# The head of a two-layer AdaLN/FFN kernel on one Trainium2 core: convolutions done directly, the first matrix loaded by another queue, end columns computed between rows of the first product

## The chip, the cores and the metric

The kernel runs on one core of one Trainium2 chip. The metric is device time in microseconds, from launch to the end of the execution. The kernel before was timed in four runs: 958.36, 963.05, 961.65 and 954.70 us, median 960.0 us.

## The reference, cut to what matters

The input is 32 samples of 64 channels and 1024 columns. Two layers follow one another. Each layer modulates the input with a small four-stage convolution net whose weights depend on a style vector, feeds the result to a matrix product, and adds that to its input:

```python
for i, typ in enumerate(('same', 'upsample', 'same', 'downsample')):
    s = style @ mw.T + mb                       # 32 x 64
    weight = SCALE * w * s[:, None, :, None]
    demod = rsqrt(sum(weight * weight, axis=(2, 3)) + EPS)
    weight = weight * demod[:, :, None, None]   # 3 taps, 64 -> 64 channels, one set per sample
    out = conv(out, weight) + b                 # 'same': 3 taps, pad 1; the two others blur as well
...
x = x + L0_ffn(L0_cond(x, cond))   # scores, top 16 of 64 experts, rank-16 products A and B
x = x + L1_ffn(L1_cond(x, cond))   # 1024 x 1024 product with int4 weights
```

In layer 0 the product with `A` (1024 x 1024) and with the router `Wr` (1024 x 64) is one product with a matrix of `AW` = 1088 columns. The 16 best scores of 64 gate its result before the product with `B`.

## The kernel before, in words

Two samples make a pair: its 2 x 64 channels lie in 128 partitions, and they are the 128 rows of the pair's token matrix. There are `NP` = 16 pairs, and every pair goes through the same stages in each layer.

**The convolution net of one sample.** The four stages are folded into two. `first` is the first convolution. A sample's 1024 columns lie twice in 128 partitions, once shifted, so that one product covers two taps. Before, a sample is first turned by `differences` into a middle part scaled by the style and two differences with its neighbours (one ACT and two DVE instructions that read every fourth column, L637 to L641). `first` then makes three products (L659, L665), moves the middle one out with ACT (`yt`, L661), joins the other two to it on DVE (L666), takes further differences on DVE (L671) and differences of these on POOL (L674). All this saves products in `rest`, which is the second, third and fourth stage composed into one: six products into one bank (L701, L709), two additions on DVE (L717, L723), four products into a second bank (L732), and a sum on DVE. The weights of `rest` are made per pair: `composed1` (`r`, then `g`, L546 to L568) and `composed2` (`f`, L579; copies L594 to L597; sums of them L599, L605).

**The product of layer 0.** `layer0` multiplies the token matrix `th` of a pair (8 chunks of 128 rows) with the 8 blocks of A. The blocks are split into high and low parts (`split_weights`, L148, L351 to L353: DVE, POOL and ACT work for each block), and every later pair uses three products of these parts. The first two pairs, `WHOLE = (0, 1)`, use A as it was loaded in plain f32 (`araw`), so that the splits can be made beside them. Their 24 products of 352 or 368 columns run block by block (`ks`), with places (`yield`) between the blocks where other work is put: `later` is `rest` of the next pair, `conv` is `first` of the pair after it.

**The ends.** The composed weights are not right for the outermost columns. `ends` computes these for all 16 pairs at once from eight columns at each side (`xg`), in a chain `xe`, `ye`, `ue`, `ze`, `ve`, `bt`, `re`, `rt`, in which TensorE and VectorE take turns. The result goes to DRAM (`red`). For pairs 0 and 1 `outer` puts it into rows 0 and 127 of `th`, in chunks 0, 1, 6 and 7, by DMA; for the others `re` is read back and merged in `rest`.

**The head.** Everything before the first product of pair 2 is written out by hand at the bottom of the function: the order there, with `tc.issue_after(...)` as anchors, is the order in which the engines get their instructions; each engine runs its own list in order. `factors` makes style, demodulation and tables; `rows` and `tbl` spread two rows of each sample over the partitions (L326, L331, L341). SP (SyncE) issues the loads of x and the small loads, POOL issues the loads of A (L365, L366). `araw` lies in rooms 5 to 7 of the weight blocks, pair 1's `y` in room 4, and the scratch of `ends` in room 2, which block 2 of the split A takes later.

Of the kernel before, what the change touches and what calls it, by code (L numbers as in the profile page):

```python
# [62 lines left out]
def adaln_ffn_kernel(ctx: ExitStack, tc: tile.TileContext, t, out: bass.AP):  # L63
# [90 lines left out]
    WHOLE = (0, 1)  # L154

# [166 lines left out]
    def last_rows(i, k, v):  # L322


        ps = mpst(f"rows{i}_{k}")
        nc.tensor.transpose(ps[:B, :C], v[:C], ident[:C, :C])  # L326
        nc.scalar.copy(rows[:, k], ps[:B, :C])
        if i == 0:
            ps = fpst(f"rows{i}_{k}b")[:, : 4 * C].rearrange("p (n c) -> p n c", n=4)
            for n in range(4):  # L330
                nc.tensor.matmul(  # L331
                    ps[:, n],
                    ident[:B, n : n + 1].to_broadcast([B, P]),
                    rows[:, k],
                    start=True,
                    stop=True,
                )
            for p in WHOLE:
                if k == 0:
                    tbl[i, p] = wk.tile([P, 2, 2, C], F32, tag="tbl", name=f"tbl{i}_{p}", bufs=3)  # L340
                nc.scalar.copy(tbl[i, p][:, :, k], ps[:, 2 * p : 2 * p + 2])  # L341


    def split_weights(raw, w, ks, into, name):

        for k in ks:
            ws = block(k, [P, 3, w], F32R, f"{name}{k}")
            for c in range(0, w, H):
                cs = slice(c, min(c + H, w))
                h = high(raw[k][:, cs], f"{name}h{k}_{c}")  # L350
                nc.gpsimd.tensor_tensor(ws[:, 1, cs], raw[k][:, cs], h, ALU.subtract)  # L351
                nc.scalar.copy(ws[:, 0, cs], h)  # L352
            nc.vector.scalar_tensor_tensor(  # L353
                ws[:, 2], ws[:, 1], -RADIX, ws[:, 0], ALU.mult, ALU.add
            )
            into.append(ws)

    def load_a():

        raw = []  # L360
        wr = t["wrT"].rearrange("(s q) e -> s q e", q=NC)
        av = t["aT"].rearrange("(s q) f -> s q f", q=NC)
        for n, (a, b) in enumerate(((0, 3), (3, 6), (6, 8))):
            r = block(5 + n, [P, 3, AW], F32, f"araw{n}")
            nc.gpsimd.dma_start(r[:, : b - a, :E], wr[:, a:b])  # L365
            nc.gpsimd.dma_start(r[:, : b - a, E:], av[:, a:b])  # L366
            raw += [r[:, j] for j in range(b - a)]
        return raw
# [40 lines left out]
    def ends(i, lo, hi, room, behind=()):  # L409
# [92 lines left out]
        if i == 1:  # L502
            yield
# [10 lines left out]
        if i == 1:  # L514
            yield
# [55 lines left out]
    def composed2(i, p, g):  # L571

        ps = mpst(f"f{i}_{p}")
        pv = ps.rearrange("p (n c) -> p n c", n=4)
        gv = g.rearrange("p k h c -> p k (h c)")
        steps = ((3, 1, 0), (1, 2, 0), (5, 0, 0), (4, 1, 1), (2, 2, 1), (0, 3, 1))
        for m, (e, n, k) in enumerate(steps):
            v = gv[:, 0::2] if k == 0 else gv[:, 1:2]
            done["f"] = nc.tensor.matmul(  # L579
                pv[:, n : n + 2 - k],  # L580
                iw[:, e].rearrange("p a b -> p (a b)"),
                v,
                start=(m == 0),
                stop=(m == len(steps) - 1),
                skip_group_check=True,
            )
        pv = ps.rearrange("p (n h c) -> p n h c", n=4, h=2)
        fw = []
        for h in range(2):

            f = fwv(h)
            once = i == 0 and p == 0
            f8 = f[:, : 8 * C].rearrange("p (k c) -> p k c", c=C)
            nc.scalar.copy(f8[:, 0::2], pv[:, :, h])  # L594
            copy = nc.vector.tensor_copy if once else nc.scalar.copy
            copy(f8[:C, 1::2], pv[C:, :, h])
            copy(f8[C:, 1:7:2], pv[:C, 1:, h])  # L597
            v = f[:, : 4 * P].rearrange("p (a two b) -> p a two b", two=2, b=P)
            (nc.vector if once else nc.gpsimd).tensor_tensor(  # L599
                f[:, 4 * P : 6 * P].rearrange("p (a b) -> p a b", b=P),  # L600
                v[:, :, 0],
                v[:, :, 1],
                ALU.add,
            )
            done["sum"] = nc.gpsimd.tensor_tensor(  # L605
                f[:, 6 * P :], f[:, : 2 * P], f[:, 2 * P : 4 * P], ALU.add
            )
            fw.append(f)
        return fw
# [12 lines left out]
    def load_x(i, n):  # L622


        if i == 0:
            xd = xdv(n)
            src = t["x"][n // 2, halves[n % 2], :]
            nc.sync.dma_start(xd[:C, 2 : L + 2], src)
            done["x"] = nc.sync.dma_start(xd[C:, 1 : L + 1], src)
            return xd[:, 2 : L + 3 : 4], xd[:, 0 : L + 1 : 4], xd[:, 4 : L + 1 : 4]  # L630
# [20 lines left out]
    def first(i, n, y):  # L651

        a = al0[:, n : n + 1]
        xe = xev(n)
        w = c0 if i == 0 else xdv(n)[:, : 3 * P].rearrange("p (a b) -> p a b", a=3)
        mid = cpst(f"c{i}_{n}_1")[:, :HQ]
        nc.tensor.matmul(mid, w[:, 1], xe[:, :HQ], start=True, stop=True)  # L659
        yt = wk.tile([P, HQ], F32, tag="yt", name=f"yt{i}_{n}", bufs=2)  # L660
        nc.scalar.activation(yt, mid, AF.Identity, bias=be0[:, n : n + 1], scale=a)  # L661
        yb, yo = y[:, :HQ], y[:, YO : YO + HQ + 1]
        for q, w_, d, o in ((0, HQ, yb, 2 * HQ - 1), (2, HQ - 1, yo[:, 1:HQ], HQ)):
            ps = cpst(f"c{i}_{n}_{q}")[:, :w_]
            done["c"] = nc.tensor.matmul(ps, w[:, q], xe[:, o : o + w_], start=True, stop=True)  # L665
            nc.vector.scalar_tensor_tensor(d, ps, a, yt[:, :w_], ALU.mult, ALU.add)  # L666
        nc.vector.memset(yb[:C, 0:1], 0.0)
        nc.vector.memset(yb[C:, HQ - 1 : HQ], 0.0)
# [4 lines left out]
        for k in range(2):  # L673
            nc.gpsimd.tensor_tensor(  # L674
                e[:, :, k], d[:, :, 2 * k : 2 * k + HQ - 2 : 2], d[:, :, 1 : HQ - 1 : 2], ALU.subtract
            )
        return y

    def rest(i, n, y, f):
# [12 lines left out]
        both = wk.tile([P, 4 * HQ], F32, tag="rt", name=f"rt{i}_{n}", bufs=1)  # L692
# [3 lines left out]

        d = y[:, YD:YO].rearrange("p (a b) -> p a b", a=2)
# [42 lines left out]
        def shape(v):  # L740
            return v.rearrange("p (k c) -> p k c", c=C)

        if whole:
            done["r0"] = nc.vector.tensor_tensor(th, shape(ps), shape(both[:, :H]), ALU.add)
            return
# [70 lines left out]
    def layer0(p, ws):  # L816
# [52 lines left out]
        if whole:  # L869


            three = [chunk(c) for c in range(3)]
            ks = (2, 3, 4, 5, 0, 1, 6, 7) if p == 0 else tuple(range(NC))
            for n, k in enumerate(ks):
                for ch in three:
                    product(ch, key, ws, at, Q, (k,), ks[0], ks[-1])
                if n in (1, 2, 4, 5, 6):
# [191 lines left out]
    def load(k, h=None):  # L1069
        if k < len(todo):  # L1070
            i, p = todo[k]
            for h in range(2) if h is None else (h,):
                xin.setdefault(k, []).append(load_x(i, 2 * p + h))
# [9 lines left out]
    def begin(k):  # L1083
        if k < len(todo):
# [11 lines left out]
    def conv(k, h, y=None):  # L1096
        if k < len(todo):
            i, n = todo[k][0], 2 * todo[k][1] + h
            y = yv(n) if y is None else y
            ys.setdefault(k, []).append(first(i, n, y))  # L1100
# [16 lines left out]
    nc.sync.dma_start(condT, t["condT"])  # L1117
    zeros_once()
    set0 = factors(0, *(block(k, [P, 3 * AW], F32, f"room{k}") for k in range(2)))
    next(set0)  # L1120
    clear(0)
    room4 = block(4, [P, 3 * AW], F32, "room4")
    y1 = [room4[:, h * Y : (h + 1) * Y] for h in range(2)]
    clear_y([yv(0), yv(1)] + y1)
    load(0)
    with tc.issue_after(done["x"].ins):
        for s, c in enumerate((0, L - 8)):
            nc.sync.dma_start(xg[:, :, s], t["x"][:, :, c : c + 8].rearrange("n p w -> p n w"))
    for _ in range(2):
        next(set0)  # L1130
    with tc.issue_after(done["blur"].ins):
        begin(0)
        compose(0)
        for h in range(2):
            conv(0, h)
    anchors = [done["xe"]]
    load(1)
    weights(0)
    with tc.issue_after(done["f"].ins):
        next(set0)  # L1140
    with tc.issue_after(done["sum"].ins):
        araw = load_a()
    with tc.issue_after(done["f"].ins):
        begin(1)
        compose(1)
        for h in range(2):
            conv(1, h, y1[h])
    with tc.issue_after(done["c"].ins):
        run(set0)
    set_ends = ends(0, 0, NP, block(2, [P, 3 * AW], F32, "room2"), anchors)  # L1150
    for h in range(2):
        next(set_ends)
        later(0, h)
        anchors.append(done["r0"])
    run(set_ends)
    outer(0)
    load(2)
    tables_of(2)
    behind = [done[v].ins for v in ("re", "r0")]
    with ExitStack() as stack:  # L1160
        for v in behind:
            stack.enter_context(tc.issue_after(v))
        weights(1)

    wa, wb, braw = [], [], []
    for k in range(NP):
# [4 lines left out]
        if k + 2 < NP:  # L1171
# [12 lines left out]
        if k == 0:  # L1184
            with ExitStack() as stack:
                for v in behind:
                    stack.enter_context(tc.issue_after(v))
                split_weights(araw, AW, range(5), wa, "wa")
        if k + 3 < NP and not ahead:
            load(k + 3)  # L1190
            tables_of(k + 3)
        beside = [[] for _ in range(5)]
        if not ahead and not last:
            beside[1] += [(later, k + 1, 0)]
            beside[3] += [(later, k + 1, 1)]
            if k + 2 < NP:
                beside[2] += [(conv, k + 2, 0), (compose, k + 2)]
                beside[4] += [(conv, k + 2, 1)]
        if k == 1:
# [159 lines left out]
```

## Time and profile before

| what | value |
|---|---|
| median of four runs | 960.0 us (954.7 to 963.05) |
| the profiled execution, its own time | 958.36 us |
| span of its instructions | 956.6 us |
| PE (TensorE matmul) busy | 884.9 us, 93% of the span |
| DVE (VectorE) | 725.9 us, 76% |
| POOL (GpSimd) | 470.1 us, 49% |
| ACT (ScalarE) | 323.8 us, 34% |
| first load of A issued, first product of pair 0 started | 29.7 us, 44.9 us |
| first product of pair 2 (split A) started | 135.7 us |

How to read it: times are microseconds from the start of the span. PE is the engine that does the products, PEld its weight loads, which overlap. A line such as L806 is a line of the kernel. In a list of waits, "PE r L701 <- POOL cv L599" says that TensorE's product at L701 stood still until POOL's instruction at L599 was done. PEclk is the share of its full clock that TensorE was granted. An f32 product counts as two instructions.

### The profile page before, as it was taken

The numbers are of one execution on the slowest core, as the hardware profiler recorded it, in microseconds if no ns is written. First come the engines' busy times: TensorE is split into PE (matmuls) and PEld (weight loads), VectorE is DVE, ScalarE is ACT, GpSimd is POOL, SyncE is SP. The second block draws the span as 40 slices with busy tenths as digits, with TensorE's granted clock in tenths as the row PEclk, the third lists the DMA queues.
The fourth block names the chain that finished last, engine by engine and source line by source line (L and its number), as shares of the span: only waits on it lengthen the run. The fifth ranks groups of instructions, "written<-read, shape, count | busy, mean of one in ns | idle before, by whom it ended". The sixth has DMA issues, their size and how long they took to land.

```text
span 956.6 us, 14770 instructions
## 1 busy us (share of the span) xinstructions
PE 884.9 (93%) x5069; PEld 785.8 (82%) x5069; DVE 725.9 (76%) x1505; ACT 323.8 (34%) x702; POOL 470.1 (49%) x601
## 2 busy tenths in 40 slices
PE   5778879999999999999999999988899999989996
PEld 4656669999999999984778887778899899988886
DVE  6856886878877788657986666588878887888885
ACT  4224442443443333332332221263233323332320
POOL 4455463444555544455662221334756655665563
PEclk9898989999999999999999999999999999999999
DMA  5721121222222221344455655464323332333221
GB/s 122 234 59 50 50 70 52 83 80 76 72 72 82 91 87 68 111 172 128 150 201 201 223 198 197 157 220 134 105 89 103 103 122 90 105 100 122 83 84 44
DMA packets 48443, 109.81 MB, mean 115 GB/s; under 512 B 12580, under 2 KB 20896, under 8 KB 48368
## 3 DMA queue, kind: packets, MB, share of 16 engines
q1 hardware_dynamic: 46208, 103.42, 34.7%
q0 software_dynamic: 1200, 4.46, 1.4%
q10 hardware_dynamic: 960, 0.99, 0.4%
q8 instruction: 40, 0.66, 0.3%
q14 instruction: 35, 0.29, 0.1%
HBM read 70.97 MB, written 37.88 MB: 114 GB/s over the span
## 4 chain that ended last, share of the span: by engine, by line
PE 27%; DVE 16%; issue 5%; POOL 3%; ACT 3%; DMA 2%; ACTq 0%; SPq 0%; POOLq 0%; DVEq 0%
PE o L806 13%; PE q L1039 5%; DVE cv L671 2%; PE f L579 2%; DVE cv L666 2%; PE c L665 1%; DVE o L1055 1%; PE r L701 1%; DVE rt L723 1%; DMA x1e<-dd 1%; DVE r L747 1%; PE r L732 1%; DVE r L546 1%; DVE r L746 1%; PE ht L922 1%
## 5 line engine op out<-in xcount | busy, mean ns | idle before, releaser
L674 POOL TENSOR_TENSOR cv<-cv 128x256 f32<-128x256 f32 x124 | 82.7, 667 | 126.4 <-DVE su L849 76.0
L774 ACT CAST thx<-h 128x512 fp32r<-128x512 f32 x60 | 37.1, 618 | 155.1 <-DVE h L148 154.9
L671 DVE TENSOR_TENSOR cv<-cv 128x257 f32<-128x257 f32 x124 | 80.4, 682 | 0.6
L666 DVE SCALAR_TENSOR_TENSOR cv<-c,al,yt 128x257 f32<-128x257 f32 x124 | 56.6, 476 | 31.0 <-ACT yt L661 29.6
L1039 PE MATMUL q<-wq,thx 128*128 128x342 f32 x384 | 74.1, 336 | 5.6 <-ACT thx L774 5.6
L701 PE MATMUL r<-cv 128*128 128x128 f32 x496 | 70.2, 284 | 9.5 <-POOL cv L599 7.8
L701 PEld LDWEIGHTS r<-cv 128*128 128x128 f32 x496 | 66.6, 198 | 12.3 <-POOL cv L599 8.5
L717 DVE TENSOR_TENSOR rt<-r,tbl 128x256 f32<-128x256 f32 x64 | 26.5, 414 | 63.5 <-PE r L709 60.3
L661 ACT ACTIVATE yt<-c,be,al 128x257 f32<-128x257 f32 x64 | 36.3, 567 | 109.1 <-PE c L659 102.6
L1039 PE MATMUL q<-wq,tlx 128*128 128x342 f32 x384 | 72.7, 332 | 0.0
L806 PE MATMUL h<-wa,tdx 128*128 128x352 f32 (+1 forms) x336 | 70.8, 349 | 0.0
L579 PE MATMUL f<-gs,iw 128*128 128x128 f32 (+1 forms) x384 | 69.7, 329 | 0.0
L599 POOL TENSOR_TENSOR cv<-cv 128x256 f32<-128x256 f32 x62 | 45.8, 738 | 47.3 <-ACT cv L597 43.9
L579 PEld LDWEIGHTS f<-gs,iw 128*128 128x128 f32 x384 | 63.4, 193 | 6.7 <-issue 0.8
L1039 PEld LDWEIGHTS q<-wq,thx 128*128 128x128 f32 x384 | 61.4, 191 | 7.6 <-ACT thx L774 7.0
L1058 POOL TENSOR_TENSOR o<-o,sc 128x342 f32<-128x342 f32 (+1 forms) x48 | 48.2, 1004 | 39.0 <-DVE sc L1057 31.5
L732 PE MATMUL r<-cv 128*128 128x128 f32 x496 | 65.5, 274 | 0.0
L806 PE MATMUL h<-wa,thx 128*128 128x352 f32 (+1 forms) x336 | 64.4, 333 | 0.0
L786 POOL TENSOR_TENSOR tdx<-thx,tlx 128x1024 fp32r<-128x1024 f32 x14 | 37.2, 2654 | 52.9 <-ACT tlx L778 48.1
L1039 PEld LDWEIGHTS q<-wq,tlx 128*128 128x128 f32 x384 | 62.5, 191 | 0.7
L806 PE MATMUL h<-wa,tlx 128*128 128x352 f32 (+1 forms) x336 | 62.4, 327 | 0.0
L806 PE MATMUL o<-wb,thh 128*128 128x512 f32 x224 | 59.8, 397 | 1.0 <-ACT wb L352 0.7
(302 smaller groups left out, 2150.5 us busy)
## 6 DMA issues: line engine op xcount, KB each, us to landing
cv<-in_x_dram SPq DMA_DIRECT2D x64, 256.0 KB
cv<-x1e SPq DMA_DIRECT2D x64, 192.5 KB
x1e<-dd SPq DMA_DIRECT2D x16, 514.0 KB
hgd<-hs SPq DMA_DIRECT2D x16, 512.0 KB
hg<-hgd SPq DMA_DIRECT2D x16, 512.0 KB
x1d<-x SPq DMA_DIRECT2D x16, 512.0 KB
xb<-x1d SPq DMA_DIRECT2D x16, 512.0 KB
out_dram<-o SPq DMA_DIRECT2D x16, 512.0 KB
```

Of the source, the lines that this page charges most:

```text
L579: done["f"] = nc.tensor.matmul(pv[:, n : n + 2 - k], iw[:, e].rearrange("p a b -> p (a b)"), v, start=(m == 0), stop=(m == len(steps) - 1) ...
L599: (nc.vector if once else nc.gpsimd).tensor_tensor(f[:, 4 * P : 6 * P].rearrange("p (a b) -> p a b", b=P), v[:, :, 0], v[:, :, 1], ALU.add,)
L666: nc.vector.scalar_tensor_tensor(d, ps, a, yt[:, :w_], ALU.mult, ALU.add)
L671: nc.vector.tensor_tensor(d[:, k], yo[:, k : k + HQ], yb, ALU.subtract)
L674: nc.gpsimd.tensor_tensor(e[:, :, k], d[:, :, 2 * k : 2 * k + HQ - 2 : 2], d[:, :, 1 : HQ - 1 : 2], ALU.subtract)
L701: nc.tensor.matmul(ps[:, j * P : (j + 1) * P], y[:, j + k : j + k + 2 * P - 1 : 2], w(4 + k), start=(k == 0), stop=(k == 1),)
L732: done["r"] = nc.tensor.matmul(ps[:, j * P : (j + 1) * P], y[:, YE + (2 * q + k) * P : YE + (2 * q + k + 1) * P], w(q + 2 * k), start=True ...
L774: nc.scalar.copy(hi, h)
L786: done["td"] = nc.gpsimd.tensor_tensor(*(v.rearrange("p a b -> p (a b)") for v in (td, *toks[key])), ALU.subtract)
L806: nc.tensor.matmul(banks[l == 2], toks[key][l][:, order(k)], w[:, cols], start=(k == first and l != 1), stop=(k == last and l in (2, min(n ...
L1039: nc.tensor.matmul(ps, half[:, k], wq[at(k)][:, c * QC : (c + 1) * QC], start=(k == 0 and j == 0), stop=(k == NC - 1 and j == 1),)
L1058: nc.gpsimd.tensor_tensor(o[:, cs], o[:, cs], s, ALU.add)
```

## The change

- `DIRECT = 4`: for pairs 0 to 3 of layer 0, `first` reads the loaded x itself. The style goes into the weights (`cm`, one ACT instruction per sample), four products per sample (two for even, two for odd outputs, accumulated in a bank) replace three, and ACT moves both banks out. `differences` isn't run for these pairs.
- For pairs 0 and 1, `rest` is sixteen products into one bank and one addition on DVE. The differences of `first` (L671, L674) and the sums of weights (L599, L605) aren't made for them.
- A is loaded on SP's queue, in the order in which the blocks are used (2, 3, 4, then 5, then 0, 1, then 6, 7), after the loads of x. Pair 1's x has a room of its own and is loaded together with pair 0's.
- `ends` stops at two more places. Its first two parts come ahead of the first product, and the others stand at the stops between blocks of pair 0's product. `outer(0)` and `outer_of(2)` follow it there. The splits of A no longer wait for the ends, but for pair 0's `rest` alone, and begin with block 3.
- Both f32 products take the blocks in the order 2, 3, 4, 5, 0, 1, 6, 7 and have their stops after blocks 1, 2, 3, 4 and 6 of that order.

```diff
+    DIRECT = 4
 ...
     def load_a():
 ...
-        for n, (a, b) in enumerate(((0, 3), (3, 6), (6, 8))):
+        for n, parts in enumerate((((2, 5),), ((5, 6), (0, 2)), ((6, 8),))):
             r = block(5 + n, [P, 3, AW], F32, f"araw{n}")
-            nc.gpsimd.dma_start(r[:, : b - a, :E], wr[:, a:b])
-            nc.gpsimd.dma_start(r[:, : b - a, E:], av[:, a:b])
-            raw += [r[:, j] for j in range(b - a)]
+            j = 0
+            for a, b in parts:
+                nc.sync.dma_start(r[:, j : j + b - a, E:], av[:, a:b])
+                nc.sync.dma_start(r[:, j : j + b - a, :E], wr[:, a:b])
 ...
+    def first(i, n, y, x):
 ...
+        if i == 0 and p < DIRECT:
+            w = wk.tile([P, 2, P], F32, tag="cm", name=f"cm{n}", bufs=2)
+            nc.scalar.activation(w, c0[:, 0::2], AF.Copy, scale=sty0[:, n : n + 1])
+            mid, before, behind = x
+            for q, d, v in ((0, yb, before), (2, yo[:, 1:HQ], behind)):
+                ps = cpst(f"c{i}_{n}_{q}")[:, : d.shape[1]]
+                nc.tensor.matmul(ps, w[:, 1 - q // 2], mid[:, : d.shape[1]], start=True, stop=False)
+                done["c"] = nc.tensor.matmul(ps, w[:, q // 2], v, start=False, stop=True)
+                nc.scalar.activation(d, ps, AF.Identity, bias=be0[:, n : n + 1], scale=a)
+            nc.vector.memset(yb[:C, 0:1], 0.0)
+            nc.vector.memset(yb[C:, HQ - 1 : HQ], 0.0)
+            if p in WHOLE:
+                return yb, yo
+            differences_of(y)
+            return y
 ...
     def rest(i, n, y, f):
 ...
+        if whole:
+            yb, yo = y
+            ps = cpst(f"r{i}_{n}")
+            for j in range(4):
+                for k in range(4):
+                    v = (yo, yb)[(j + k) % 2]
+                    o = j // 2 + k // 2 + (j % 2) * (k % 2)
+                    done["r"] = nc.tensor.matmul(
+                        ps[:, j * P : (j + 1) * P], v[:, o : o + 2 * P - 1 : 2], w(k),
+                        start=(k == 0), stop=(k == 3),
+                    )
+            c = tbl[i, p][:, h, 1].unsqueeze(1).to_broadcast([P, 2 * 4, C])
+            done["r0"] = nc.vector.tensor_tensor(th, shape(ps), c, ALU.add)
+            return
 ...
     def layer0(p, ws):
 ...
-            ks = (2, 3, 4, 5, 0, 1, 6, 7) if p == 0 else tuple(range(NC))
+            ks = (2, 3, 4, 5, 0, 1, 6, 7)
 ...
-                if n in (1, 2, 4, 5, 6):
+                if n in (0, 1, 2, 3, 5):
                     yield
 ...
     load(0)
+    load(1, rooms=x1)
     with tc.issue_after(done["x"].ins):
-        for s, c in enumerate((0, L - 8)):
-            nc.sync.dma_start(xg[:, :, s], t["x"][:, :, c : c + 8].rearrange("n p w -> p n w"))
+        araw = load_a()
+    for s, c in enumerate((0, L - 8)):
+        nc.sync.dma_start(xg[:, :, s], t["x"][:, :, c : c + 8].rearrange("n p w -> p n w"))
 ...
+    set_ends = ends(0, 0, NP, block(2, [P, 3 * AW], F32, "room2"))
+    next(set_ends)
+    next(set_ends)
 ...
         if k == 0:
-            with ExitStack() as stack:
-                for v in behind:
-                    stack.enter_context(tc.issue_after(v))
-                split_weights(araw, AW, range(5), wa, "wa")
+            with tc.issue_after(done["r0"].ins):
+                split_weights(araw, AW, (3, 0, 1, 2, 4), wa, "wa")
 ...
+        if k == 0:
+            beside[0] += [(next, set_ends)]
+            beside[2] += [(next, set_ends)]
+            beside[3] += [(run, set_ends), (outer, 0), (outer_of, 2)]
```

## The prediction

> **What bounds the kernel now.** I read first the slices of the page, then stages of the span, then TensorE's waits.
>
> The page cuts the span into 40 slices of 23.9 us; a digit is the busy share of a slice in tenths.
>
> ```profile
> PE   5778879999999999999999999988899999989996
> ...
> PEclk9898989999999999999999999999999999999999
> ```
>
> TensorE is full from the seventh slice on. What it loses lies in the first six, the head, and there its clock is cut as well. The stages, with busy times of each engine, the granted clock and the DMA share:
>
> ```profile
> 0.00:15.00 15.00, 4.92 (x21) 4.25 (x21) 7.87 (x25) 8.07 (x20) 7.76 (x36) 1.00 0.66 130
> 15.00:45.00 30.00, 26.05 (x126) 21.46 (x127) 25.34 (x69) 9.20 (x23) 14.13 (x20) 0.89 0.67 193
> 45.00:65.00 20.00, 14.84 (x61) 10.10 (x62) 9.14 (x23) 5.55 (x14) 8.94 (x9) 0.91 0.40 108
> 65.00:90.00 25.00, 19.97 (x81) 14.28 (x80) 21.24 (x43) 10.19 (x20) 13.72 (x15) 0.86 0.12 31
> 90.00:115.00 25.00, 24.58 (x118) 18.42 (x117) 16.46 (x35) 8.95 (x20) 10.88 (x14) 1.00 0.23 65
> 115.00:139.30 24.30, 14.40 (x81) 12.15 (x80) 20.56 (x43) 11.49 (x29) 17.86 (x19) 0.86 0.16 49
> 139.30:420.00 280.70, 280.70 (x1770) 268.66 (x1769) 213.31 (x540) 106.73 (x224) 128.42 (x146) 1.00 0.28 87
> ```
>
> From 15 to 139.3 us TensorE is busy 26.05 + 14.84 + 19.97 + 24.58 + 14.40 = 99.8 of 124.3 us, so idle 24.5. Part of the busy time is slow clock: 0.11 x 26.05 + 0.09 x 14.84 + 0.14 x 19.97 + 0.14 x 14.40 = 9.0 us. From 139.3 to 420 us it is never idle. The point 139.3 is a part of pair 2's first product (the low half of its tokens, L806). From it on, the two kernels' instruction lists are the same on all five engines, to the end. So the change is worth what it moves this point by, and nothing behind it has slack to swallow the move. What TensorE waits for from 14 to 140 us (sum, times, longest):
>
> ```profile
> PE r L701 <- POOL cv L599: 9.2, 2, 7.8
> ...
> PE c L665 <- DVE rt L723: 4.5, 3, 2.5
> PE c L665 <- DVE thx L744: 2.4, 1, 2.4
> PE re L507 <- DVE room L479: 2.2, 1, 2.2
> ...
> PE h L806 <- DVE thx L744: 1.6, 1, 1.6
> PE h L806 <- DMA araw<-in_aT_dram: 1.5, 1, 1.5
> ```
>
> No single wait rules: the convolution's banks wait for DVE, `rest` waits for POOL's sums, the product for tokens and for A.
>
> **The change, part by part.** *Direct `first`, pairs 0 to 3.* TensorE gets four products per sample for three. A 257-column product follows the one before by 0.43 us (21.07 to 21.50 in the timeline), so 8 samples x 0.43 = +3.4 us. Off DVE go the two strided differences (0.68 and 0.66 us) and two joins (0.476 each, the L666 group), 2.3 us a sample, 18 us in all. ACT swaps one 0.757 us (L637) for `cm` of much the same size, and one 0.567 us eviction for two: 8 x 0.57 = 4.5 us more, on an engine that is busy 45 of the 124 us. That takes away the waits of `c` on DVE: 4.5, 2.4 and four under 1 us, about 9.5 us.
>
> *The unknown price: strided reads.* The four products stream x with a step of four columns, 16 bytes; before they streamed packed tiles. No product of this trace does that. Lower bound: TensorE's split product streams 368 columns in 0.166 us (eight follow in 1.33 us at 152.28), 0.45 ns a column, while an f32 product takes 0.84 ns a column and pass (0.43 us over 2 x 257). A read twice as slow, 0.90 ns, would stretch it by 7%: 32 products x 0.43 x 0.07 = 1.0 us. Upper bound: ACT needs 0.757 us for 257 strided columns (L637), 0.567 us for packed ones (L661), and on DVE the strided L638 takes 684 ns where L671 takes 420, so at most a doubling, 32 x 0.43 = 13.8 us. I take the lower, because TensorE's own row is the nearest, and keep 13.8 for the range. [...]
>
> *Direct `rest`, pairs 0 and 1.* Sixteen products for ten, at 0.235 us (four of L701 in 0.94 us, 76.21 to 77.15): 4 x 6 x 0.235 = +5.6 us of TensorE. Off go, per sample, two DVE additions (0.42 and 0.68), two differences on DVE (0.42) and two on POOL (0.67), and POOL's sums for these pairs (0.73 each): the first wait on L599 (1.4 us) has no cause left.
>
> *A by SP.* POOL's six issues (29.71 to 34.4 us) go; SP gets eight at about 0.5 us, as its x loads show. They stand behind x of both pairs. The 5.5 MB of x and A at the 300 GB/s of the stretch 34 to 52 us take 18 us from 14 us on, so A is in by about 33 us; its first use is at 41. The wait on `araw` (1.5) goes. Behind them on SP stand `rowd`, pair 2's x and its table, which are needed after 50 us.
>
> *A new wait.* The multiplications for `xe` (L440, before at 24.57 us without any wait) now stand in DVE's list ahead of the blur additions and the reciprocal (L265, ended at 14.07). They wait for `xg`, whose 32-byte packets run until 13.4 us. Behind them stand the reciprocal, `al0`, the table rows, and with these ACT's evictions of the first convolutions: about 3 us later. TensorE has the direct products of pair 0 to do meanwhile, so 2 us of idle remain.
>
> *Ends between blocks.* The chain's DVE turns now stand among the splits (L148, L353), which wait for POOL: a block costs POOL 2 x 1.265 + 0.32 = 2.85 us. Following the lists at the durations above: `rest` of pair 0 starts at 27, the first product at 41 (before 44.9), `ye` is joined only at 47, so `ue` keeps TensorE 1.5 us; `rt` is there at 61.5, and its four DMAs (0.6 us each on SP after `red`, 1.2) land by 66.5 to 68, just as block 0 is due: 0.4 us. The wait of `re` (2.2) goes, since a part of the product stands ahead.
>
> *Behind pair 0.* Pair 0's product ends at 74 (before 87.4). The gates' table load and exponential stand on ACT ahead of two evictions, and DVE's last split ahead of the gates: 1.6 us for a bank. POOL then has gates before pair 2's sums: 1.0 us. Pair 1's product ends at 104 (before 115.4), and POOL reaches pair 3's sums at 102 to 103, so the 7.8 us wait goes; some 1.5 us remain around `g` and `f` of pair 4.
>
> *The sum.* New idle: 2 + 1.5 + 0.4 + 1.6 + 1.0 + 1.5 = 8 us instead of 24.5: -16.5. Slow clock in the same proportion: 9.0 x 8 / 24.5 = 3 instead of 9: -6. The row for that: in 24 to 28 us TensorE is busy 2.3 of 4 us, and from 28 to 34 the granted clock is 0.50. [...] Work on TensorE: +3.4 + 5.6 + 1.0 = +10.0. Together -12.5 us: 958.4 - 12.5 = 945.9 for the profiled execution. The median of the runs lies 1.6 higher, so 947.5.
>
> **Rivals.** *Strided reads cost double on TensorE* (its price 12.8 above what I took): the gain is eaten up, 960.3 on the median. For it: both ACT and DVE show it; against: f32 products ask for an element only every 0.84 ns. Chance 0.16.
>
> *Waits come back elsewhere.* DVE, POOL and ACT run in order, and each handed-on microsecond that I followed at its median may be longer. With 16 us of idle instead of 8 and 6 us of slow clock instead of 3, the gain is 1.5 us: 958.5. For it: DVE was 85% busy from 65 to 90 us; against: 18 us of DVE work are gone. Chance 0.13.
>
> *The splits set the pace, and the kernel is slower.* POOL's split subtractions now run ahead of the ends, the gates and the sums, and everything there goes through them. Fourteen 512-wide ones lie before the point. At their median, 1.265 us, I have them covered; the longest took 2.25 and 2.30. It decides from 12.5 / 14 = 0.9 us more each, 2.15 us. If all took 2.3 and the seven joins (L353) 1.8 instead of 1.28, that is 14.5 + 3.6 = 18.1 us: 965.6. A further stretch, by ACT and DMA landings that these waits collect, could pass 970. For it: long ones stand where DVE and POOL both work, at 58.87 and 119.61; against: the median. Chance 0.15.
>
> *The change does not do what it says:* A's DMAs could be listed ahead of `xg`, and DVE would stand until 33 us. In the built list `xg` is ahead, so I give this nothing of its own.
>
> **How the numbers follow.** My case has 0.56 and its own range of 937 (no new idle and no slow clock, 8 + 3 us less) to 951. A measurement of this kernel can tell about 1%, that is 950.4 and 969.6. Nearly all of my case lies below 950.4, and I give faster 0.55; strided reads, returned waits and half of the slow-split case fall within 1%: 0.33; slower 0.12. The range takes in that low end and the strided bound: 937 to 962.
>
> **What would show it.** Pair 0's first product near 41 us and pair 2's low-half product (the point at 139.3) near 127; `c` products of pairs 0 to 3 following at 0.43 us (0.86 if strides cost double); DVE standing at `xg` until about 14 us; no wait of the first product on A; waits on L599's successor under 2 us; the granted clock at 0.5 in fewer stretches. A first product later than 45 us, or POOL subtractions of over 2 us throughout, would make the prediction wrong; so would any difference in the length of the span behind the point.

## The result, and the profile after

The changed kernel takes 962.1 us in the median of 45 runs (958.3 to 965.6); the kernel before, run beside it, 961.2 us. The ratio is 1.0011 with a 95% interval of 1.0000 to 1.0021: no gain, at most a fifth of a per cent of loss. The forecast was 947.5 us.

The slices of the page after, TensorE's busy tenths and its granted clock:

```profile
PE   5988989999999999999999999988999899999996
...
PEclk9999999999999999999999999999999999999997
```

The head has filled up, and no slice there has a mean granted clock under 9 tenths any more (inside the second slice it still falls to 0.50, from about 23.1 to 26.5 us). Yet nothing got shorter. The stages, with columns as in the prediction (busy time of TensorE, its weight loads, DVE, ACT, POOL; clock; DMA share; GB/s), the last one cut at the low-half product that the prediction took as its point (before at 139.30, now at 140.01):

```profile
15.00:45.00 30.00, 28.89 (x131) 21.11 (x131) 9.53 (x36) 9.45 (x26) 1.79 (x4) 0.94 0.68 211
45.00:65.00 20.00, 16.07 (x94) 12.91 (x94) 15.14 (x25) 6.43 (x16) 8.85 (x9) 1.00 0.05 13
65.00:90.00 25.00, 25.00 (x108) 17.10 (x107) 10.93 (x25) 8.05 (x17) 9.27 (x10) 1.00 0.19 50
90.00:115.00 25.00, 22.36 (x93) 14.41 (x92) 15.31 (x37) 11.41 (x23) 10.76 (x14) 1.00 0.22 66
115.00:140.01 25.01, 20.61 (x105) 16.11 (x103) 19.71 (x42) 11.85 (x31) 15.32 (x19) 0.93 0.26 72
```

TensorE is busy 112.9 of 125.0 us, so it idles 12.1 us instead of 24.5. Slow clock is 0.06 x 28.89 + 0.07 x 20.61 = 3.2 us instead of 9.0. But busy time at full clock is 109.7 us instead of 99.8 - 9.0 = 90.8: 18.9 us more work where the prediction had 10.0. The account closes: +18.9 - 12.4 - 5.8 = +0.7 us, which is the move of the point. Waits did go away, and work took their place.

Which work, the timeline of TensorE says (start, length, line, tiles; x2 because an f32 product is two instructions):

```profile
65.54 1.07 PE L687 MATMUL c<-cv,cm 128*128 128x257 f32 x2
66.43 1.09 PE L688 MATMUL c<-cv,cm 128*128 128x257 f32 x2
67.34 1.08 PE L687 MATMUL c<-cv,cm 128*128 128x256 f32 x2
```

The direct products follow one another by 0.90 us, where packed ones took 0.43. There are 32 of them. What TensorE waits for now (14 to 145 us; sum, times, longest):

```profile
PE f L586 <- ACT gs L575: 3.5, 1, 3.5
PE ue L477 <- DVE room L433: 2.3, 1, 2.3
PE h L852 <- ACT hs L871: 1.7, 1, 1.7
PE ye L458 <- ACT cv L604: 1.6, 1, 1.6
...
PE r L753 <- POOL cv L609: 1.0, 1, 1.0
```

The long waits of before (9.2 for POOL's sums, 4.5 and 2.4 of the convolution for DVE) are gone, and so is the product's wait for A. New at the top is `f`, the weights of pair 4, which waits for `gs`, the copy of `g` that ACT makes.

### The profile page after: what moved, and what is told of

Read it like the earlier page. It is cut to its first block, busy times and chain, and to the rows that moved or that the text cites. A ratio compares the mean times of both kernels' runs of the same rounds, so it can differ in the third digit from the quotient of the medians.

```text
span 961.1 us, 14823 instructions
## 1 busy us (share of the span) xinstructions
PE 902.9 (94%) x5133; PEld 794.6 (83%) x5133; DVE 703.7 (73%) x1455; ACT 326.3 (34%) x710; POOL 450.4 (47%) x583
## 4 chain that ended last, share of the span: by engine, by line
PE 27%; DVE 15%; issue 4%; DMA 3%; ACT 3%; POOL 3%; ACTq 0%; SPq 0%; POOLq 0%; DVEq 0%
PE o L852 12%; PE q L1084 6%; PE f L586 2%; DVE cv L664 2%; DVE cv L705 1%; PE c L704 1%; PE r L753 1%; DVE o L1100 1%; DVE r L793 1%; PE r L784 1%; DMA x1e<-dd 1%; DVE rt L775 1%; DVE x L1012 1%; DVE r L553 1%; DVE sc L1102 1%
## 5 line engine op out<-in xcount | busy, mean ns | idle before, releaser
L667 POOL TENSOR_TENSOR cv<-cv 128x256 f32<-128x256 f32 x120 | 79.7, 664 | 122.9 <-DVE su L895 69.3
L705 DVE SCALAR_TENSOR_TENSOR cv<-c,al,yt 128x257 f32<-128x257 f32 x112 | 51.1, 477 | 31.1 <-ACT yt L701 29.8
L753 PE MATMUL r<-cv 128*128 128x128 f32 x480 | 67.6, 284 | 3.1 <-POOL xg L1055 1.9
L753 PEld LDWEIGHTS r<-cv 128*128 128x128 f32 x480 | 63.7, 197 | 6.2 <-POOL cv L609 2.3
L701 ACT ACTIVATE yt<-c,be,al 128x257 f32<-128x257 f32 x56 | 31.8, 567 | 103.0 <-PE c L699 93.1
L609 POOL TENSOR_TENSOR cv<-cv 128x256 f32<-128x256 f32 x60 | 44.2, 737 | 48.0 <-ACT cv L604 39.7
L784 PE MATMUL r<-cv 128*128 128x128 f32 x480 | 64.2, 277 | 0.0
```

What stands on the lines that cost most here:

```text
L609: nc.gpsimd.tensor_tensor(f[:, 4 * P : 6 * P].rearrange("p (a b) -> p a b", b=P), v[:, :, 0], v[:, :, 1], ALU.add,)
L667: nc.gpsimd.tensor_tensor(e[:, :, k], d[:, :, 2 * k : 2 * k + HQ - 2 : 2], d[:, :, 1 : HQ - 1 : 2], ALU.subtract)
L753: nc.tensor.matmul(ps[:, j * P : (j + 1) * P], y[:, j + k : j + k + 2 * P - 1 : 2], w(4 + k), start=(k == 0), stop=(k == 1),)
L784: done["r"] = nc.tensor.matmul(ps[:, j * P : (j + 1) * P], y[:, YE + (2 * q + k) * P : YE + (2 * q + k + 1) * P], w(q + 2 * k), start=True ...
```

## The experiments

Each kernel is the changed one with the edit shown, unless another is named. "The point" is the start of the 368-column product that follows the low-half one: 140.45 us before, 141.30 after. Behind it the listed instructions are the same in before and after, but one execution's stretch from the point to the end of the span lay between 813.8 and 819.8 us in the thirteen profiles; so the point tells more than one profile's span, and for the whole the medians count. The two do not agree everywhere. For the changed kernel, e1 and e6 they lie within 1 us of one another, but e3, e4, e5, e7, e8, e9 and e10 gain 1.2 to 2.9 us more by their medians (6 to 10 runs) than by their points. The intervals of the medians are as wide as that, and no run shows where it comes from.

**e1_packed: the same products, packed reads.** The direct products of the first four pairs read columns that lie side by side instead of the right ones.

```diff
+            if n < 2 * DIRECT:
+                return xd[:, 2 : 2 + HQ], xd[:, 300 : 300 + HQ], xd[:, 600 : 600 + HQ - 1]
             return xd[:, 2 : L + 3 : 4], xd[:, 0 : L + 1 : 4], xd[:, 4 : L + 1 : 4]
```

> The changed kernel, with the four products of the direct first convolution (pairs 0 to 3) reading packed columns instead of every fourth one. It reads other columns of x than it should, so the output of the eight samples is not the reference's; sizes, counts, loads and order are as in the changed kernel. Theory 'stride': TensorE reads a 16-byte step at half speed; the 32 products follow each other at 0.43 us instead of 0.905, 15 us less work, and since TensorE's idle time before the common point is only 12 us, most of that comes out in the end: 12 us faster than the changed kernel, about 949 where the kernel before has 961. Rival 'returned waits': the products are quicker, but TensorE then stands for DVE, POOL and ACT, its idle time grows from 12 to over 22 us, and the time stays at 958 to 962.

Measured: 953.6 us, ratio 0.992 (0.988 to 0.996); first product at 43.97 instead of 49.09; point at 132.61 instead of 141.30. The same stretch of the timeline:

```profile
60.42 0.60 PE L689 MATMUL c<-cv,cm 128*128 128x257 f32 x2
60.85 0.60 PE L690 MATMUL c<-cv,cm 128*128 128x257 f32 x2
```

They follow at 0.43 us. The instruction list is the changed kernel's, and with nothing else changed but where the columns lie, 8.7 us come back. So the stride is the loss. It is less than the 12 us expected: TensorE's work up to the low-half product (131.32) falls by 12.4 us, to 97.3, but idle grows from 12.1 to 14.8 us and slow clock from 3.2 to 4.3.

**e2_steps: what a step costs.** Pairs 0, 1, 2 and 3 read with steps of 1, 2, 3 and 4 columns.

```diff
+            if n < 2 * DIRECT:
+                st = n // 2 + 1
+                v = [xd[:, o : o + (HQ - 1) * st + 1 : st] for o in (2, 2, 2)]
+                return v[0], v[1], v[2][:, : HQ - 1]
```

> The changed kernel with a different step of the columns read by the direct first convolution for each pair: step 1 (4 bytes) for pair 0, step 2 (8 bytes) for pair 1, step 3 (12 bytes) for pair 2, step 4 (16 bytes) for pair 3; apart from that step it leaves the computation of the first convolution wrong for eight samples, with the same sizes and counts. Theory 'stride', as a line of 16 bytes: steps 1, 2 and 3 follow at 0.43 us a product and only step 4 at 0.90. Rival 'stride in proportion': 0.43, 0.55 to 0.6, 0.7 to 0.75, 0.9. Rival 'not the stride' (the two accumulating products, or the weights made by ACT, are slow): 0.9 in all four.

Measured: 958.17 us in a single execution. TensorE's timeline, two products of each of the pairs 1, 2 and 3:

```profile
27.40 0.61 PE L692 MATMUL c<-room,cm 128*128 128x257 f32 x2
27.86 0.61 PE L691 MATMUL c<-room,cm 128*128 128x256 f32 x2
...
60.91 0.84 PE L691 MATMUL c<-cv,cm 128*128 128x257 f32 x2
61.58 0.85 PE L692 MATMUL c<-cv,cm 128*128 128x257 f32 x2
...
95.14 1.07 PE L691 MATMUL c<-cv,cm 128*128 128x257 f32 x2
96.03 1.09 PE L692 MATMUL c<-cv,cm 128*128 128x257 f32 x2
```

By the starts (with the later ones of each pair) 0.455, 0.68 and 0.90 us; packed 0.43 (pair 0's last one as well, 21.67 to 22.10). So neither the two accumulating products nor the weights made by ACT are slow, and the expectation "only step 4" fell too. For each column and pass (2 x 257) that is 0.84, 0.88, 1.32 and 1.76 ns. Steps 2, 3 and 4 stand as 2 to 3 to 4, by 0.44 ns for each column of the step. Two readings were left: the cost goes on growing with the step, or it stops at 16 bytes, where step 4 already is.

**e11_long_steps: in proportion, or an end at 16 bytes?** Samples 4 to 7 read with steps of 8, 6, 5 and 16 columns, 256 columns in rows of 128 (of 64 for 16).

```diff
+                st = {4: 8, 5: 6, 6: 5, 7: 16}.get(n)
...
+                    m = 64 if st == 16 else 128
+                    v = xdv(n)[:, 2 : 2 + L // st * st].rearrange("p (a b) -> p b a", b=st)
+                    v = v[:, : 256 // m, :m]
```

> The changed kernel, but the direct products of samples 4, 5, 6 and 7 read x with steps of 8, 6, 5 and 16 columns (32, 24, 20 and 64 bytes): 256 columns as two rows of 128 (four of 64 for the step of 16), and one column by itself; the output of these four samples is not the reference's. From e2_steps: 0.43, 0.454, 0.678 and 0.905 us for a product of 2 x 257 columns at steps of 1 to 4, so 0.84, 0.88, 1.32 and 1.76 ns for a column. Theory A (a read costs 0.44 ns for each element that it passes over, so 0.44 ns times the step once that is above 0.84 ns): a product of 2 x 256 columns takes 1.13 us at step 5, 1.35 at 6, 1.80 at 8 and 3.60 at 16. Theory B (lines of 16 bytes, one line a read): from step 4 on nothing is added, all four take 0.90 us. What the time of the whole comes to follows: by A 16 products more by 0.2 to 2.7 us, some 10 us over 962; by B 962.

Measured: 961.49 us in a single execution, the kernel before beside it 961.57. The timeline, first the step of 8 and then that of 16:

```profile
66.09 1.08 PE L696 MATMUL c<-cv,cm 128*128 128x256 f32 x2
66.99 1.10 PE L697 MATMUL c<-cv,cm 128*128 128x256 f32 x2
...
112.06 1.02 PE L696 MATMUL c<-cv,cm 128*128 128x256 f32 x2
112.91 1.04 PE L697 MATMUL c<-cv,cm 128*128 128x256 f32 x2
```

0.90 us at 32 bytes, 0.85 at 64; 5 and 6 columns took 0.89 to 0.91. Beyond 16 bytes a longer step adds nothing: theory A falls, and the figure of theory B, 1.76 ns for each column from 16 bytes on, stands at steps 4, 5, 6 and 8. The step of 16 lies 5% below, and why is not known (its rows had 64 columns instead of 128). At the short end step 2 cost 5% over packed columns (0.88 for 0.84 ns), step 4 a factor of 2.1 (1.76). The lines of theory B are my reading of these times; that a read takes 16 bytes at once no run shows.

**e3_planar: right columns, packed.** x comes a second time with each row's four phases apart (a change of the input's layout), so that middle, left and right neighbours lie packed.

```diff
...
+            if n < 2 * DIRECT:
+                pl = xd[:, 2 : 2 + 2 * (HQ + 1)].rearrange("p (a b) -> p a b", a=2)
+                src = t["x4"][n // 2, halves[n % 2]]
+                nc.sync.dma_start(pl[:C, :, : HQ - 1], src[:, 0::2])
+                done["x"] = nc.sync.dma_start(pl[C:, :, : HQ - 1], src[:, 1::2])
+                return pl[:, 0, :HQ], xd[:, HQ + 2 : 2 * HQ + 2], pl[:, 1, : HQ - 1]
...
+        "x4": i["x"].reshape(NP, P, L // 4, 4).transpose(0, 1, 3, 2),
```

> The changed kernel with x of pairs 0 to 3 laid out phase by phase in DRAM (an input in another order), so that the direct first convolution reads packed columns and computes the right thing; its loads are half as large (two of 128 KB a sample instead of two of 256 KB, in 1 KB runs). Theory 'stride': as with packed wrong columns, 11 to 14 us faster than the changed kernel, 947 to 950, 1.1 to 1.4% below the kernel before. Rival 'returned waits': 958 to 962.

Measured: 951.84 us, ratio 0.991 (0.987 to 0.994); first product at 44.51, point at 133.62. It is faster by 0.9%, not by 1.3%. It is not the changed kernel with packed reads alone, for its instruction list differs in one more thing: SP issues `xg` at 16.8 us, behind all of A (in the changed kernel at 7.3, ahead of it), and the multiplications for `xe` stand late in DVE's list, at 33.4 us instead of 12.9:

```profile
33.38 0.25 DVE L449 TENSOR_TENSOR room<-xg,styp 128x96 f32<-128x96 f32 x1
```

So DVE doesn't stand at `xg`, and the reciprocal starts at 13.33 us instead of 16.37. That earned nothing by itself: e1_packed, where DVE stood until 14.40, has its first product at 43.97. The stages of e3_planar, the last one up to the low-half product at 132.34:

```profile
15.00:45.00 30.00, 28.79 (x160) 24.89 (x159) 9.37 (x38) 10.63 (x28) 3.66 (x6) 0.94 0.46 139
45.00:65.00 20.00, 15.59 (x85) 12.03 (x84) 14.17 (x30) 6.26 (x16) 6.79 (x8) 1.00 0.01 2
65.00:90.00 25.00, 22.34 (x108) 16.35 (x107) 10.68 (x26) 11.18 (x25) 12.61 (x17) 1.00 0.15 49
90.00:115.00 25.00, 24.37 (x125) 18.99 (x123) 20.25 (x34) 12.69 (x27) 14.74 (x16) 1.00 0.28 70
115.00:132.34 17.34, 11.37 (x51) 9.62 (x51) 13.71 (x35) 5.69 (x15) 7.70 (x11) 0.70 0.22 68
```

Busy 102.5 of 117.3 us: idle 14.9, slow clock 0.06 x 28.79 + 0.30 x 11.37 = 5.1, work at full clock 97.3. The work is that of e1_packed, 12.4 us less than in the strided kernel, but idle grows by 2.8 and slow clock by 1.9: here the shorter stage shows a wait that it hid. It is the one for `f` of pair 4:

```profile
PE f L586 <- ACT gs L575: 5.7, 1, 5.7
```

**e5_gates_first and e6_strided_gates: is that wait worth 5.7 us?** The chain behind it is long: `gs` stands on ACT behind the gates' exponential (L898 there), that one waits for the gates on DVE, and they stand in DVE's list behind the last 64 columns of block 7's split (L148), which waits 4.0 us for POOL's subtraction (L356). Both experiments list that split behind the gates, e5 on e3_planar, e6 on the changed kernel.

```diff
-            nc.vector.tensor_scalar_mul(nm, m0[:, 0:1], -1.0)
+            done["nm"] = nc.vector.tensor_scalar_mul(nm, m0[:, 0:1], -1.0)
...
-            split_weights(araw, AW, (7,), wa, "wa")
+            with tc.issue_after(done["nm"].ins):
+                split_weights(araw, AW, (7,), wa, "wa")
```

> Packed reads as in e3_planar, and block 7's split is listed behind pair 1's gates, so that the gates no longer stand behind a split that waits for POOL. Theory (the missing part of the gain is a wait that came back: f of pair 4 for gs, 5.7 us, through the gates' exponential on ACT): that wait falls to 1.5 us or less, the clock from 115 to 140 us stays at 0.9 or above, pair 2's low-half product comes 4 to 6 us earlier than in e3_planar (133.6), so at 128 to 130, and the time is 946 to 949. Rival (the work behind, POOL's sums and the split itself, is due at the same time anyway): the wait only changes its name, the point moves by less than 1.5 us and the time is 950 to 953.

> The changed kernel with its strided reads and one edit: block 7's split listed behind pair 1's gates. The wait of f for gs (3.5 us) should go and the slow clock of 115 to 140 us (1.5 us of it) with it: point at 137 to 138 instead of 141.3, time 957 to 959. By the rival (something else is due then) the point stays within 1 us and the time at 961 to 962.

Measured: e5 950.92 us, ratio 0.990 (0.986 to 0.994), point at 132.73, 0.9 us earlier than e3_planar; e6 961.85 us, ratio 1.0005 (0.998 to 1.003), point at 140.70, 0.6 earlier than the changed kernel. The waits of e5 from 14 to 145 us:

```profile
PE r L760 <- POOL cv L609: 2.5, 2, 1.5
PE ue L477 <- DVE room L433: 2.3, 1, 2.3
PE c L711 <- DVE rt L782: 2.0, 1, 2.0
PE c L711 <- ACT yt L708: 1.9, 1, 1.9
```

The wait for `gs` is gone altogether, and the point gained only 0.9 of its 5.7 us: the waits for POOL's sums, for the tokens' sum on DVE and for `yt` grew by 5.0 together. The rival was right in both. In neither kernel was the longest wait of the list a measure of what its removal gave.

**e7_pool_queue and e8_pool_ends_late: what A by SP is worth.** Both are e3_planar with A loaded by POOL in three parts in order of index, behind the `f` products of pair 0; e8 also lists `xe` behind the first sum of tokens. In both the list has `xg` early again (issued at 9.9 us), and in e7 `xe` too.

```diff
-        for n, parts in enumerate((((2, 5),), ((5, 6), (0, 2)), ((6, 8),))):
+        for n, parts in enumerate((((0, 3),), ((3, 6),), ((6, 8),))):
...
-                nc.sync.dma_start(r[:, j : j + b - a, E:], av[:, a:b])
-                nc.sync.dma_start(r[:, j : j + b - a, :E], wr[:, a:b])
+                nc.gpsimd.dma_start(r[:, j : j + b - a, :E], wr[:, a:b])
+                nc.gpsimd.dma_start(r[:, j : j + b - a, E:], av[:, a:b])
...
-    with tc.issue_after(done["x"].ins):
-        araw = load_a()
...
+    with tc.issue_after(done["f"].ins):
+        araw = load_a()
```

```diff
-    set_ends = ends(0, 0, NP, block(2, [P, 3 * AW], F32, "room2"))
+    set_ends = ends(0, 0, NP, block(2, [P, 3 * AW], F32, "room2"), [done["r0"]])
```

> As e3_planar (packed reads), but A is loaded as in the kernel before: by POOL's queue in three parts in order of index, behind the f products of pair 0. My prediction put the price of this part at the one wait of 1.5 us on A. If that is right the first product waits on A for 1 to 3 us, the point comes 1 to 3 us later than in e3_planar (133.6) and the time is 953 to 955. If the early A also feeds the splits and these set the pace, the point moves by 4 us or more, 956 or above. If nothing needs A earlier, the time stays at 951 to 953.

> e7_pool_queue with the multiplications that read xg listed behind the first sum of tokens. In e7_pool_queue the first part of A left POOL at 10.1 us, xg landed at 18.9 instead of 14.4, the reciprocal behind it ended at 22.2 and the first product stood 4.4 us later than in e3_planar. Theory (the loss of e7_pool_queue is that DVE wait, not A's arrival): the reciprocal ends at 14 to 15 again, the first product is at 44 to 45 instead of 48.9, pair 2's low-half product at 133 to 136, time 951 to 955. Rival (A on POOL is late, or its list order holds the sums of pair 3 back): the first product comes forward but the wait of r for POOL's sums (8.3 us) stays or grows, the point stays at 138 or later, time 956 to 959.

Measured: e7 958.87 us, ratio 0.998 (0.996 to 1.000), first product at 48.90, point at 140.34; e8 954.59 us, 0.995 (0.992 to 0.997), first product at 43.92, point at 136.10. DVE's timeline in e7:

```profile
14.02 0.26 DVE L449 TENSOR_TENSOR room<-xg,styp 128x96 f32<-128x96 f32 x1 [3.57 <-DMA xg<-in_x_dram]
18.99 0.26 DVE L450 TENSOR_TENSOR room<-xg,styp 128x96 f32<-128x96 f32 x1 [4.51 <-DMA xg<-in_x_dram]
```

In e7 POOL issues the first part of A at 10.1 us, beside `xg`, whose second half then lands after 18.9 us instead of 14.0 in the changed kernel. DVE stands at it, the reciprocal starts at 21.28, and all of the head shifts. With `xe` out of the way (e8, at 42.0 us) the reciprocal starts at 12.72. So of the 6.7 us between e7's point and that of e3_planar, 4.2 are this wait, though e7's time alone would have fitted the expectation that the splits set the pace. The other 2.5 are A by POOL in this order (with `xe` at 42.0 instead of 33.4), and with it stands an 8.3 us wait of `r` for POOL's sums (7.8 in the kernel before), which both e7 and e8 have. Neither kernel shows a wait of the product for A.

**e4_no_direct: without the direct first convolution.** `DIRECT = 0`; the direct `rest`, A by SP and the ends stay.

```diff
-    DIRECT = 4
+    DIRECT = 0
...
+        if i == 0 and p in WHOLE:
+            return yb, yo
...
+    begin(0)
     compose(0)
...
+    begin(1)
```

> The change without its direct first convolution: pairs 0 to 3 go through the differences on ACT and DVE again (three products a sample), while the direct later stages of pairs 0 and 1, A on SyncE's queue and the ends between blocks stay. Theory 'stride': TensorE has 8 x (3.62 - 1.29) = 18.6 us less work than in the changed kernel, DVE 18 us more, and the waits of the first convolution on DVE (9.5 us) come back: 950 to 954. Rival 'returned waits': DVE's work is what sets the head, 961 or slower.

Measured: 956.67 us, ratio 0.994 (0.992 to 0.996), point at 137.93: between the two expectations. Its interval lies clear below that of the changed kernel: on this layout of x the direct convolution costs 0.7%. Against e3_planar the intervals overlap; by the points packed reads turn that part into a gain of 4.3 us.

**e9_warm and e10_best: the slow first products.** In e3_planar the first products, from 14.2 to 17.8 us, follow at 0.855 us although packed, while the granted clock reads 1.00. e9 puts 13 transposes of the identity into TensorE's gaps ahead of them; e10 is e5_gates_first with the same.

```diff
+        if i == 0:
+            warm = cpst("warm")
+            for k in range(7):
+                nc.tensor.transpose(warm[:, :P], ident, ident)
...
+            turned = nc.tensor.transpose(ps[:, k * P : (k + 1) * P], cw[:, 2, k], ident)
+        if i == 0:
+            with tc.issue_after(turned.ins):
+                for k in range(6):
+                    nc.tensor.transpose(warm[:, P : 2 * P], ident, ident)
```

> e3_planar with 13 extra transposes of the identity on TensorE, 7 ahead of the dps products and 6 ahead of the first convolution, into a bank that nobody reads. In e3_planar the first ten convolution products follow at 0.855 us, from 14.2 us on, the later ones at 0.43, though the profile grants the full clock there; I read this as a TensorE that is still cold after the gaps of 8 to 10 and 12.6 to 14.2 us. Theory: with the gaps filled the products follow at 0.43 from the first or second on, the first product comes up to 4 us earlier than 44.5 (at 40.5 to 43, the reciprocal and the table rows then set the pace), the point at 130 to 133, time 948 to 950. Rival (the slow stretch is not set by what TensorE did before, but by operands, the x transfers that land at the same time): the products still follow at 0.855 until 18 us, first product at 44 to 45, time 951 to 953.

> e5_gates_first (packed reads, gates ahead of block 7's split) with the 13 transposes of e9_warm: the version that should beat both kernels. If the cold start counts, 946 to 949 with the point at 129 to 132; if it does not, 950 to 951 as e5_gates_first.

Measured: e9 950.07 us, ratio 0.990 (0.987 to 0.993); e10 949.31 us, 0.988 (0.984 to 0.991). TensorE's timeline in e9:

```profile
12.46 1.49 PE L279 MATMUL warm<-ident 128*128 128x128 f32 x6
14.26 1.23 PE L702 MATMUL c<-cv,cm 128*128 128x257 f32 x2 [0.31 <-ACT cm L698]
...
16.13 1.06 PE L702 MATMUL c<-cv,cm 128*128 128x256 f32 x2
16.99 0.65 PE L703 MATMUL c<-cv,cm 128*128 128x256 f32 x2
```

The gap is filled but for 0.31 us, and the products stay at 0.85 us until 17.0, in e10 until 17.5; without transposes they do until 17.3 in e1, 17.8 in e3 and 18.9 in e2. So filling these gaps does not remove the slow stretch; what ends it stays open. A second slow stretch (near 21 to 25 us), where the granted clock does read 0.50, is missing in e9 and there in e10, which explains their first products (42.38 and 44.17): two products and `g` take 1.7 us more there. That either beats e3_planar or e5_gates_first by its transposes is not shown: the intervals overlap. e10 is faster than the kernel before by 1.2%, and so than the changed one, and needs x in the second layout.

## Why the prediction was wrong, point by point

**The step that failed is the price of strided reads.** I had both bounds, 1.0 and 13.8 us, and took the lower, "because TensorE's own row is the nearest". The row was right and was read wrongly. The split product takes 0.45 ns for a packed column; I took that for the time of one read, and a strided read for one twice as slow. By e2 a column that lies 16 bytes from the last takes 1.76 ns, and by e11 no longer beyond. Four packed columns of the split product, 16 bytes as well, take 4 x 0.45 = 1.80 ns, which is near, but whether the one time follows from the other no run shows. Against the 0.84 ns of an f32 column, 1.76 is 2.1 times. So the term is 32 x (0.905 - 0.43) = 15.2 us instead of 1.0, above even my upper bound. (That bound was not clean either: the ACT and DVE rows that I compared differ in more than the step. L661 reads a product's bank, and L671 is another operation than L638.) In the account 12.4 us of it show as work, because some seven products ran in slow stretches, where packed ones take 0.855 anyway; 8.7 us (e1) or 7.7 (e3) reach the point, the rest having covered waits and slow clock. The rival "strided reads cost double on TensorE" named it, with 960.3 us; 962.1 was measured. But the rest of the sum was too low as well, and the near hit of that rival is in part luck: e3_planar pays no stride and took 951.84 us, where the sum without its 1.0 us gives 946.5. Against the sum without the stride, e3_planar has 6.9 us more idle time and 2.1 more slow clock. Its added work is 6.5 us (97.3 against 90.8), where I had 9.0; those 2.5 us are not traced.

**Idle, the second miss.** I had 8 us; there are 12.1, and 14.9 with packed reads. Right in size were the bank behind the gates' table load (1.6, measured 1.7) and POOL's sums of pair 2 (1.0 and 1.0). `ue` was 2.3 for 1.5. Not listed was `ye`, 1.6, behind ACT's copies of pair 1's weights. The 0.4 for the outer DMAs did not come. The large one is `f` and `g` of pair 4: 1.5 predicted, 3.5 measured, 5.7 with packed reads. By e5 this is no single wait but a stretch in which DVE, POOL and ACT hand over to one another with little slack. About half of the rival "waits come back elsewhere" is in this.

**The head.** The first product was to start at 41 us; it came at 49.09, and at 44.51 packed. Slow stretches (14 to 18 and 22 to 25 us in e3) are worth about these 3.5 us: some seven products by 0.42 us each, and `g` with 1.91 us instead of 1.03; e9, without the second of them, has 42.38. I took 0.43 us from a row at 21 us, while the timeline before shows, at 17.89 us, two products (four instructions) that lasted until 19.77, with a granted clock of 1.00.

**What held.** The point as a measure: it moved by 0.85 us, the median by 0.9. The slow clock: 3.2 us, predicted 3, in part by luck, since the packed kernels have 4.3 (e1) and 5.1 (e3). In the changed kernel the granted clock reads 0.50 from about 23.1 us on, with gaps of TensorE of 0.29 and 0.82 us just before; that slow clock goes in proportion to idle time was my estimate, and that the gaps bring it about no run shows. The direct `rest`: 17 products in 4.13 us at 42.31, 0.24 each, where I had 0.235. DVE at `xg`: it stood until 14.08, as said; that this costs TensorE 2 us is not shown, since e1, where it stood until 14.40, has its first product no later than e3. The price of A by POOL's queue: 1.5 us in the sum, 2.5 by e8, though not through the wait that I named. POOL's subtractions did not lengthen as a whole (median 1.271 us, a longest one of 2.31 in the changed kernel, none over 1.32 in e3_planar), so the rival of the slow splits fell. The case "A listed ahead of `xg`", to which I gave nothing, came about in e3, where it cost nothing because `xe` was listed later as well; in e7, with A beside `xg` on another queue and `xe` early, DVE stood until 18.99 and it cost 4.2 us.

## What to carry to other kernels

Price a strided moving operand (here x, with its 256 or 257 columns) by a product that reads with that step: here a column took 0.84 ns packed, 0.88, 1.32 and 1.76 ns at steps of 2, 3 and 4 columns (e2), and no more beyond (e11). The fast packed row gave the time of a column among neighbours, not that of one read: its 0.45 ns, doubled, made 0.90 where 1.76 was measured; times the four columns of the step it would have made 1.80, which is one case and no rule yet. Where two bounds lie 13 us apart and the forecast's sign hangs on them, the bound that was taken has to say why the other cannot be. And the longest wait of the list is not the gain of removing it: follow the stretch to what is due next; e5 got 0.9 us for 5.7.

## What the runs showed of the hardware that was not expected

An f32 product of 2 x 257 columns takes 0.43, 0.455, 0.68 and 0.90 us with its moving columns 4, 8, 12 and 16 bytes apart, and no more beyond (2 x 256 columns: about 0.90 at 20, 24 and 32 bytes, 0.85 at 64). While TensorE runs at half its pace the stride costs almost nothing: in the changed kernel a strided product takes 0.91 us at 15.75 and at 23.36, and 0.90 at full pace; packed ones take 0.85 and 0.86 in such stretches (e1, at 15.56 and 21.69) and 0.43 outside them. So the strided product takes the same time at either pace. The second of these stretches stands in the profile with a granted clock of 0.50 (24 to 26 us in the changed kernel), but the first, at the same half pace from 14 to between 17 and 19 us, with a granted clock of 1.00.
